# A searched order of work, and transposes and tile results in shared PSUM banks, in a three-layer mixture-of-experts and attention kernel

## The chip, the cores and the metric

The kernel runs on one core of a Trainium2 chip. The metric is device time in microseconds (us) for one execution of the whole program; lower is better. Engines: TensorE (PE, with its weight loads as PEld), VectorE (DVE), ScalarE (ACT), GpSimd (POOL) and SyncE (SP). They run side by side, each through its own queue in order, and wait for each other on semaphores.

## What is computed

```python
x = x + 0.5 * ffn(layernorm(x))
x = x + attn(layernorm(x))
x = x + 0.5 * ffn(layernorm(x))

def ffn(x):
    shared = (silu(x @ shared_gate.T) * (x @ shared_up.T)) @ shared_down.T
    probs = sigmoid(x @ router_w.T + routing_bias)
    scores, indices = top_k(probs, 2)          # of 8 experts, scores normed to sum 1
    w = scores scattered to (tokens, 8)
    g = silu(einsum('th,ehi->tei', x, gate_w)); u = einsum('th,ehi->tei', x, up_w)
    return shared + einsum('tei,eih,te->th', g * u, down_w, w)

def attn(x):                                    # 8 heads of 16, rope on q and k
    kv = einsum('bshd,bshe->bhde', k, v)        # linear attention: no S x S matrix
    num = q @ kv * scale + v.sum(1); den = q @ k.sum(1) * scale + S
    o = num / den + depthwise_conv(v, 5 taps)
    return (o * (x @ Wg.T)) @ Wo.T
```

x is 8 blocks of 512 tokens of width 128, all in float32. An expert's inner width is 256. The weights are the same in both FFNs.

## The kernel before

**Groups and tiles.** The 8 blocks go in two groups (g = 0, 1) of 4 blocks, through two FFNs (f = 0, 1) with attention between them, so there are four pairs (f, g), called groups below. For each group `route` (L449) turns the scores into a list of 39 tiles of 128 token places, each tile of one expert. `tile_lane` (L656) does a tile: GpSimd gathers its 128 rows from DRAM (`xg`), TensorE transposes them (`px`) and ACT copies them out (`xT`); one 128x512 matmul pair gives gate and up (`pgu`); ACT takes the silu (`sg`), DVE multiplies (`hh`); TensorE transposes twice (`ph`), ACT copies (`hT`); two accumulating matmuls give the tile's result (`py`), ACT copies it (`y`), and GpSimd scatters it to DRAM (`yd`). With all 39 tiles of a group done, `combine` (L728) loads the results (`yy`) and adds them, weighted, to the residual x. `shared` (L616) is the shared expert for one block: four steps of `pgu_s`, `sg_s`, `gu_s`, then eight matmuls `py_s` and an update of x. `attention` (L760) is one block's attention, and `prep` (L420) the layernorm, its transposes (`pxn`) and the router's logits (`pl`).

**What sets the order.** All these pieces are generators. A piece stops at each `Want`, which names the buffers, tensors or gate that it needs next. `run_lanes` (L206) takes, again and again, the lane with the earliest start by the planner's own clock; `rank` decides between lanes that could start at the same time. The planner's clock is `Order.note` (L80), which holds a written-in length for every kind of instruction, and `ready`, `used` and `free_at`, which say by a tile's name when it can be read and when its buffer comes free. What a lane issues is put on the engines' queues in that order; the semaphores between them follow from the tiles that instructions read and write. Ranks before are short formulas in g, f, block and tile (the last loop of the kernel).

**PSUM before.** The rings are made at L264. `gu` has 2 tiles of a whole bank (for `pgu` and `pgu_s`), `tr` 2 tiles of half a bank each (for `px` and `ph`), `y` one tile (for `py`), and `side` 3 banks for all else. In the built program each of these tiles has a bank of its own: 2 + 2 + 1 + 3 = 8.

```python
    for tag, bufs, shape, space in (
        ("gu", 2, [P, 2 * I], PSUM), ("tr", 2, [P, 2 * P], PSUM), ("y", 1, [P, D], PSUM),
        ("side", 3, [P, S], PSUM), ("xg", 8, [P, D], None), ("xT", 3, [P, P], None),
...
            rank = lane.rank if lane.want.rank is None else lane.want.rank
            key = (max(t, now), rank)
```

Nearly all instructions are issued through one helper, `Eng.call`, and so have line 158 in the profile; they are told apart by their tiles' names.

Of the kernel before, what the change touches and what calls it, by code (L numbers as in the profile page):

```python
# [8 lines left out]
F32 = mybir.dt.float32  # L9
# [25 lines left out]
EW = 2 * I + NI * D  # L35


SHORT = {"DVE": 2.5, "POOL": 2.0}


class Order:
# [3 lines left out]
    def __init__(self):  # L45
        self.t = {"PE": 0.0, "DVE": 0.0, "ACT": 0.0, "POOL": 0.0, "SP": 0.0,
                  "bytes": 0.0}
        self.ready, self.used, self.rings, self.open = {}, {}, {}, set()
        self.by = {}
        self.mark = 0.0  # L50
        self.table = None


    def ring(self, tag, pool, bufs, shape):
        self.rings[tag] = [pool, bufs, shape, []]

    def free_at(self, tag):
        _, bufs, _, names = self.rings[tag]
# [7 lines left out]
    def take(self, tag, name):  # L66
        pool, bufs, shape, names = self.rings[tag]
        at = self.free_at(tag)
        assert at is not None, (tag, name)
        t = pool.tile(shape, F32, tag=tag, name=name)  # L70
        names.append(t.tensor.name)
        self.open.add(t.tensor.name)
        self.used[t.tensor.name] = at
        return t

    def free(self, *tiles):
        for t in tiles:
            self.open.remove(t.tensor.name)

    def note(self, eng, op, a, k):  # L80
        aps = [v for v in list(a) + list(k.values()) if isinstance(v, bass.AP)]
        out, ins = aps[0], aps[1:]
        if k.get("out") is not None:
            out = k["out"]
            ins = [v for v in aps if v is not out]
        for v in k.values():
            if isinstance(v, bass.IndirectOffsetOnAxis):
                ins.append(v.ap)
        n = 1
        for d in out.shape[1:]:  # L90
            n *= d
        lag = 0.15
        if eng == "PE":
            if op == "transpose":
                cost = 0.125
            elif ins[0].dtype != F32:
                cost = 0.08
            else:
                cost = max(0.25, 0.00168 * n)
        elif op == "dma_start":  # L100
            cost, lag = 0.08, 2.2
        elif op == "indirect_dma_start":
            cost, lag = 1.25, 1.6
        elif eng == "DVE":
            cost = 0.13 + (0.0006 if out.dtype not in (F32, mybir.dt.int32) else 0.00105) * n
            if op == "bn_stats":
                cost = 0.2
            elif op == "bn_aggr":
                cost = 0.08
            elif op == "scalar_tensor_tensor":  # L110
                cost += 0.08
            elif op == "tensor_reduce":
                cost = 0.36 if ins[0].shape[-1] > 1 else 0.25
        elif eng == "ACT":
            cost = 0.16 + 0.00083 * n
            if op == "activation" and k.get("bias") is not None:
                cost += 0.12
            f = a[2] if op == "activation" and len(a) > 2 else None
            if f in (AF.Silu, AF.Sigmoid) and f != self.table:
                cost += 1.3  # L120
                self.table = f
        else:
            cost = 1.03 if op == "tensor_tensor" else 0.2
        start = self.t[eng]
        for v in ins:
            name = v.tensor.name
            who, end = self.by.get(name, (None, 0.0))
            start = max(start, end if who == eng else self.ready.get(name, 0.0))
        o = out.tensor.name
# [12 lines left out]
        for v in ins:  # L142
            nm = v.tensor.name
            self.used[nm] = max(self.used.get(nm, 0.0), end + 0.1)
        self.mark = max(self.mark, end + lag)

# [27 lines left out]
class Lane:  # L174


    def __init__(self, rank, gen, behind=None):
        self.rank, self.gen, self.want, self.marked = rank, gen, Want(), 0.0
        self.behind = behind

    def at(self, order):

        w = self.want
        if w.gate is not None and not w.gate():
            return None
        t = self.marked if w.mark else 0.0
        for tag in w.tags:
            f = order.free_at(tag)
            if f is None:
                return None  # L190
            t = max(t, f)
        for v in w.on:
            t = max(t, order.ready.get(v.tensor.name, 0.0))
        q = w.queue or self.behind
        if q:
            t = max(t, order.t[q] - SHORT[q])
        return t

    def step(self, order):
        order.mark = 0.0  # L200
        self.want = next(self.gen, None)
        self.marked = order.mark
        return self.want is not None


def run_lanes(order, lanes):  # L206


    while lanes:
        now = order.t["PE"]  # L210
        best = None
        for lane in lanes:
            t = lane.at(order)
            if t is None:
                continue
            rank = lane.rank if lane.want.rank is None else lane.want.rank
            key = (max(t, now), rank)
# [9 lines left out]
def kernel(  # L227
# [34 lines left out]
    pe, dve, act = Eng(od, nc.tensor, "PE"), Eng(od, nc.vector, "DVE"), Eng(od, nc.scalar, "ACT")  # L262
    pool, sp = Eng(od, nc.gpsimd, "POOL"), Eng(od, nc.sync, "SP")
    for tag, bufs, shape, space in (  # L264
        ("gu", 2, [P, 2 * I], PSUM), ("tr", 2, [P, 2 * P], PSUM), ("y", 1, [P, D], PSUM),
        ("side", 3, [P, S], PSUM), ("xg", 8, [P, D], None), ("xT", 3, [P, P], None),
        ("sg", 3, [P, I], None), ("hh", 3, [P, I], None), ("hT", 3, [P, NI * P], None),
        ("ys", 5, [P, D], None),
    ):
        kw = {"space": space} if space else {}  # L270
        od.ring(tag, ctx.enter_context(tc.tile_pool(name=f"r_{tag}", bufs=bufs, **kw)), bufs, shape)


    xres = [const.tile([P, C, D], F32, tag=f"x{b}", name=f"x{b}") for b in range(NB)]
# [341 lines left out]
    def shared(G, bl, turn):  # L616
        b = G.g * GB + bl
        u = f"s{G.u}_{bl}"
        yield Want(gate=lambda: bl in G.xnT and len(finished) >= turn - 1 and groups[0, 0].scored
                   and (G.f == 0 or groups[1, NG - 1].prepared == GB))  # L620
        xnT = G.xnT[bl]
        yield Want("gu", "sg", on=[xnT])
        gu = keep.tile([P, NI, S], F32, tag="sgu", name=f"gu_{u}", bufs=2)
# [291 lines left out]
    def in_stage(n, bl, gen):  # L915
        yield Want(gate=lambda: stage[bl] == n)
        yield from gen
        stage[bl] += 1

    def first_prep(g, bl):  # L920
        yield Want(on=[xres[g * GB + bl]], gate=lambda: g == 0 or groups[0, 0].begun >= LEAD + 4 * bl)
        yield from prep(groups[0, g], bl)

    def middle(g, bl):

        yield from combine(groups[0, g], bl)
# [12 lines left out]

    lanes = [Lane(0, q_lane())]  # L940
    for g in range(NG):
        for f in range(2):
            G = groups[f, g]
            lanes.append(Lane(5 + g, route(G, 2 * f + g)))
            for j in range(NT):
                lanes.append(Lane(40 + 2 * (2 * f + g) + j / NT, tile_lane(G, j)))
        for bl in range(GB):
            lanes.append(Lane(10 + 60 * g + bl, in_stage(g, bl, first_prep(g, bl))))
            lanes.append(Lane(20 + 4 * g + bl, in_stage(NG + g, bl, middle(g, bl)), "DVE"))
            lanes.append(Lane(60 + 4 * g + bl, in_stage(2 * NG + g, bl, out_lane(g, bl))))  # L950
# [72 lines left out]
```

## Time and profile before

| what | value |
|---|---|
| median of 3 runs | 645.43 us (642.58 to 649.0) |
| the profiled execution's own time | 648.35 us |
| its span in the profile | 646.6 us |
| mean granted TensorE clock | 0.917 |
| indirect transfers issued by GpSimd | 312 (156 gathers, 156 scatters) |
| first gather | starts at 42.9 us |
| loads of a group's results (yy), by group | from 186.8, 331.2, 509.3 and 628.9 us |

The page lists busy time by engine, the span in 40 slices (busy tenths, and the granted clock of TensorE in tenths), and the chain of work that ended last, followed back from the end. "issue" is time in which an engine waited for nothing that the profile shows. Other views give the waits by who waited for whom, the busy time in chosen stretches, and the instructions in order of time. Durations there come from the one profiled execution.

### The profile page before, as it was taken

What the parts mean: (1) busy time and instruction counts of PE and PEld (TensorE: products, weight loads), DVE (VectorE), ACT (ScalarE), POOL (GpSimd) and SP (SyncE); (2) the same over time, 40 slices, a digit from 0 to 9 for tenths busy, and PEclk for the clock granted to TensorE, in tenths of its full rate; (3) what the DMA queues carried; (4) which work ended last, traced back from release to release, by engine and by line L of the source; (5) the groups of instructions that cost most, each with busy time, mean ns of one, the idle gap of its engine ahead of it and who ended that gap; (6) DMA issues with size and microseconds to landing.
All of it is one profiled execution on the core that took longest, in us unless ns stands there. A gap on an engine that the chain in (4) does not pass through costs nothing.

```text
span 646.6 us, 9387 instructions
## 1 busy us (share of the span) xinstructions
PE 518.8 (80%) x2668; PEld 369.4 (57%) x2668; DVE 315.9 (49%) x1014; ACT 293.8 (45%) x933; POOL 347.2 (54%) x353
## 2 busy tenths in 40 slices
PE   3777979778889999997647889989686877887793
PEld 3565756455665767675334467667364655555573
DVE  5573222273227678773545677782562243232235
ACT  1214446533446665454405655454533444453343
POOL 5026566656665666466355455356456656566530
PEclk9989788997899999998766999997789979899997
DMA  9802122111141112112141011102111421111206
GB/s 247 230 13 58 33 57 68 38 35 37 38 148 48 38 32 58 33 53 48 18 147 40 14 33 45 36 28 65 30 29 46 155 61 58 48 50 46 41 15 190
DMA packets 41825, 40.59 MB, mean 63 GB/s; under 512 B 7085, under 2 KB 37049, under 8 KB 41776
## 3 DMA queue, kind: packets, MB, share of 16 engines
q0 software_dynamic: 9984, 18.65, 11.2%
q1 hardware_dynamic: 30944, 20.95, 10.8%
q10 hardware_dynamic: 848, 0.40, 0.3%
q8 instruction: 23, 0.38, 0.2%
q14 instruction: 26, 0.21, 0.1%
HBM read 25.28 MB, written 16.52 MB: 65 GB/s over the span
## 4 chain that ended last, share of the span: by engine, by line
PE 65%; DVE 11%; issue 9%; ACT 8%; DMA 3%; another core or an unknown queue 2%; POOL 1%; DVEq 0%; SPq 0%; ACTq 0%; POOLq 0%
PE pgu L158 20%; PE py L158 11%; PE pgu_s L158 7%; PE ph L158 6%; PE px L158 4%; PE py_s L158 3%; PE pl_f L158 3%; PE pkv L158 2%; DMA xg<-xnd,idx 2%; ACT hT L158 1%; PE pf L158 1%; PE pxn_f L158 1%; PE pi L158 1%; PE pkk L158 1%
## 5 line engine op out<-in xcount | busy, mean ns | idle before, releaser
L158 POOL DMA_INDIRECT yd<-y,dst x156 | 161.0, 1032 | 153.9 <-ACT y L158 87.7
L158 POOL DMA_INDIRECT xg<-xnd,idx x156 | 156.3, 1002 | 78.8 <-issue 35.0
L158 PE MATMUL pgu<-wx,xT 128*128 x312 | 180.9, 670 | 13.8 <-issue 8.7
L158 PEld LDWEIGHTS py<-wx,hT 128*128 128x128 f32 x624 | 95.5, 206 | 91.1 <-issue 41.8
L158 DVE TENSOR_TENSOR hh<-pgu,sg 128x256 f32<-128x256 f32 x156 | 65.2, 423 | 161.1 <-ACT sg L158 109.9
L158 PE MATMUL py<-wx,hT 128*128 x624 | 108.0, 299 | 35.2 <-issue 18.0
L158 ACT ACTIVATE sg<-pgu 128x256 f32<-128x256 f32 x156 | 60.0, 386 | 87.6 <-PE pgu L158 63.3
L158 ACT COPY hT<-ph 128x256 f32<-128x256 f32 x156 | 56.9, 371 | 48.7 <-PE ph L158 20.6
L158 ACT COPY y<-py 128x128 f32<-128x128 f32 x156 | 41.4, 265 | 75.0 <-PE py L158 33.9
L158 PEld LDWEIGHTS pgu<-wx,xT 128*128 128x128 f32 x312 | 53.6, 212 | 24.9 <-issue 16.8
L158 PE MATMUL ph<-ident,hh 128*128 128x128 f32 x312 | 62.3, 291 | 6.6 <-ACT xT L158 5.1
L158 PE MATMUL px<-ident,xg 128*128 128x128 f32 x156 | 40.3, 299 | 32.6 <-ACT hT L158 17.9
L158 PEld LDWEIGHTS ph<-ident,hh 128*128 128x128 f32 x312 | 43.0, 153 | 36.4 <-issue 18.7
L158 DVE TENSOR_TENSOR gu_s<-pgu_s,sg_s 128x256 f32<-128x256 f32 x64 | 26.7, 423 | 75.9 <-ACT sg_s L158 50.1
L158 PEld LDWEIGHTS px<-ident,xg 128*128 128x128 f32 x156 | 22.6, 150 | 53.2 <-ACT hT L158 24.2
L158 ACT COPY xT<-px 128x128 f32<-128x128 f32 x156 | 38.8, 273 | 21.6 <-PE px L158 15.0
L158 ACT ACTIVATE sg_s<-pgu_s 128x256 f32<-128x256 f32 x64 | 24.4, 384 | 52.2 <-PE pgu_s L158 23.5
L158 PE MATMUL pgu_s<-xnT_f,sgw 128*128 128x256 f32 x128 | 41.9, 411 | 0.6 <-DVE hh L158 0.2
L158 PE MATMUL pgu_s<-xnT_f,suw 128*128 128x256 f32 x128 | 40.4, 399 | 0.0
L158 POOL TENSOR_TENSOR rstd_f<-ve_f,neghalf 128x4 f32<-128x4 f32 x16 | 16.7, 1044 | 33.6 <-DVE ve_f L158 31.6
L158 PE MATMUL py_s<-sdw,gu_s 128*128 128x128 f32 x256 | 31.9, 277 | 1.6 <-DVE gu_s L158 1.6
L158 PEld LDWEIGHTS py_s<-sdw,gu_s 128*128 128x128 f32 x256 | 30.6, 194 | 2.6 <-DVE gu_s L158 1.8
(143 smaller groups left out, 656.9 us busy)
## 6 DMA issues: line engine op xcount, KB each, us to landing
yy<-yd SPq DMA_DIRECT2D x16, 512.0 KB
xnd<-xn_f SPq DMA_DIRECT2D x16, 256.0 KB
xg<-xnd,idx POOLq DMA_INDIRECT x156
yd<-y,dst POOLq DMA_INDIRECT x156
x<-in_x_dram SPq DMA_DIRECT2D x8, 256.0 KB
out_dram<-x SPq DMA_DIRECT2D x8, 256.0 KB
wx<-in_gate_w_dram SPq DMA_DIRECT2D x1, 1024.0 KB
wx<-in_up_w_dram SPq DMA_DIRECT2D x1, 1024.0 KB
```

The costliest lines, as they stand in the source:

```text
L158: r = f(*a, **k)
```

## The change

Three things are changed together.

1. **PSUM.** `gu` gets a third bank. The banks of `tr` and `y` go; two banks, `bank0` and `bank1`, take their place. `tr` becomes a ring of three places of half a bank: both halves of bank 0 and the first half of bank 1. `y` becomes a ring of two places, the third and fourth quarter of bank 1. `Order` keeps such a place's state by the place (`name`, `ring_of`), not by the bank.
2. **Ranks.** Every lane takes its rank from a table, and for tiles, shared blocks and the middle lanes each piece of a lane can add to it (`ADD`). The tables are numbers found by trial.
3. **Gates.** A shared block starts only when a number of tiles from `AFTER` has begun (for the eight blocks of the second FFN 122, 120, 68, 42, 84, 128, 41 and 115, for those of the first 0, 0, 0, 0, 13, 1, 31 and 0). The old gate, that the second FFN's shared blocks wait until the last group's blocks are prepared, goes. The order of the shared blocks among each other stays bound by `len(finished) >= turn - 1`, so the blocks of the second FFN, behind the first two gates, start when 120 tiles have begun.

The planner's lengths for GpSimd's elementwise work also change a little. What each instruction computes is the same, and so is the number of instructions.

```diff
+RANK = {
+    "q_lane": [
+        -62.33,
+    ],
+    "route": [
+        42.26, -96.58, 12.75, -83.93,
+    ],
...
+AFTER = [
+    0, 122, 0, 120, 0, 68, 0, 42, 13, 84, 1, 128, 31, 41, 0, 115,
+]
...
+    def ring_of(self, tag, places):
+
+        for t, first, _ in places:
+            self.shared.setdefault(t.tensor.name, []).append([first, None])
+            self.shared[t.tensor.name].sort(key=lambda part: part[0])
+        self.rings[tag] = [None, len(places), places, []]
+
+    def name(self, v):
+
+        parts = self.shared.get(v.tensor.name)
+        if parts is None:
+            return v.tensor.name
+        return [who for first, who in parts if first <= v.offset % S][-1]
...
-        t = pool.tile(shape, F32, tag=tag, name=name)
-        names.append(t.tensor.name)
-        self.open.add(t.tensor.name)
-        self.used[t.tensor.name] = at
+        if pool is None:
+            tensor, first, n = shape[len(names) % bufs]
+            t = tensor[:, first : first + n]
+            for part in self.shared[tensor.tensor.name]:
+                if part[0] == first:
+                    part[1] = name
+        else:
+            t = pool.tile(shape, F32, tag=tag, name=name)
+            name = t.tensor.name
+        names.append(name)
+        self.open.add(name)
+        self.used[name] = at
         return t
...
-            cost = 1.03 if op == "tensor_tensor" else 0.2
+            cost = 1.03 if n < 100 else 0.21 + 0.00207 * n
...
+    def rank_now(self):
+        own = self.rank if self.want.rank is None else self.want.rank
+        return own + (self.add[self.n] if self.n < len(self.add) else 0.0)
...
-        ("gu", 2, [P, 2 * I], PSUM), ("tr", 2, [P, 2 * P], PSUM), ("y", 1, [P, D], PSUM),
+        ("gu", 3, [P, 2 * I], PSUM),
...
+    bank = ctx.enter_context(tc.tile_pool(name="bank", bufs=1, space=PSUM))
+    banks = [bank.tile([P, S], F32, tag=f"b{n}", name=f"bank{n}") for n in range(2)]
+    od.ring_of("tr", [(banks[n // 2], n % 2 * 2 * P, 2 * P) for n in range(3)])
+    od.ring_of("y", [(banks[-1], 2 * P, P), (banks[-1], 3 * P, P)])
...
-        yield Want(gate=lambda: bl in G.xnT and len(finished) >= turn - 1 and groups[0, 0].scored
-                   and (G.f == 0 or groups[1, NG - 1].prepared == GB))
+        yield Want(gate=lambda: bl in G.xnT and len(finished) >= turn - 1 and groups[0, 0].scored)
...
-                lanes.append(Lane(40 + 2 * (2 * f + g) + j / NT, tile_lane(G, j)))
+                lanes.append(
+                    Lane(tiles_at[f * NG + g] + j / 40, tile_lane(G, j), add=ADD["tile"])
+                )
...
-                lanes.append(Lane(80 + 8 * f + 4 * g + bl, shared(groups[f, g], bl, (f * NG + g) * GB + bl)))
+                lanes.append(
+                    Lane(next(rank["shared"]), shared(groups[f, g], bl, (f * NG + g) * GB + bl),
+                         add=ADD["shared"], gate=begun(next(after)))
+                )
```

More of the change, by code (lines that the diff above doesn't have):

```diff
@@ L35 @@
 EW = 2 * I + NI * D
-SHORT = {"DVE": 2.5, "POOL": 2.0}
+RANK = {
[5 more added lines that the diff above has]
+    ],
+    "first": [
+        -10.65, -4.01, -21.58, -57.52, 51.38, 69.46, 67.86, 85.67,
+    ],
+    "mid": [
+        18.79, 11.7, 26.03, 28.66, 38.54, 25.61, 27.43, 11.7,
+    ],
+    "out": [
+        42.09, 4.55, 59.73, 122.09, 132.48, -14.93, -0.46, 83.82,
+    ],
+    "shared": [
+        80.65, 88.09, 59.59, 89.79, 60.46, 97.66, 135.22, 101.96, 65.72, 55.98, 94.12, 171.42,
+        91.54, 79.83, 98.56, 67.09,
+    ],
+    "tile": [
+        16, 43.86, 78.77, 52.12,
+    ],
+}
+ADD = {
+    "mid": [
+        0, 4.12, 0, 1.19, 0, -33.91, -9.15, -70.78, 1.76, -1.4, -0.73, 0.87, -7.22, -12.47,
+        14.32, 0, 0.49, -31.74, 0, 0.26, 2.81, -1.33, -2.51, 13.43, -0.86, -44.2, -0.06, -0.94,
+        0, -2.24, -11.81, 46.28,
+    ],
+    "tile": [
+        0, 0.33, -40.05, 0, 0, 0, 13.55, 0,
+    ],
+    "shared": [
+        0, -0.16, 0, -11.33, 4.43, -0.01, -1.23, -2.28,
+    ],
+}
+AFTER = [
+    0, 122, 0, 120, 0, 68, 0, 42, 13, 84, 1, 128, 31, 41, 0, 115,
+]
+SHORT = {"DVE": 2.5, "POOL": 2}
 class Order:
@@ L49, in __init__ @@
         self.by = {}
+        self.shared = {}
         self.mark = 0.0
@@ L77, in free, with busy @@
         for t in tiles:
-            self.open.remove(t.tensor.name)
+            self.open.remove(self.name(t))
+    def busy(self, eng, op, cost):
+        self.t[eng] += cost
     def note(self, eng, op, a, k):
@@ L122, in note @@
         else:
-            cost = 1.03 if op == "tensor_tensor" else 0.2
+            cost = 1.03 if n < 100 else 0.21 + 0.00207 * n
         start = self.t[eng]
         for v in ins:
-            name = v.tensor.name
+            name = self.name(v)
             who, end = self.by.get(name, (None, 0.0))
             start = max(start, end if who == eng else self.ready.get(name, 0.0))
-        o = out.tensor.name
+        o = self.name(out)
         start = max(start, self.used.get(o, 0.0))
@@ L142, in note @@
         for v in ins:
-            nm = v.tensor.name
+            nm = self.name(v)
             self.used[nm] = max(self.used.get(nm, 0.0), end + 0.1)
@@ L174, with __init__ @@
 class Lane:
-    def __init__(self, rank, gen, behind=None):
+    def __init__(self, rank, gen, behind=None, add=(), gate=None):
         self.rank, self.gen, self.want, self.marked = rank, gen, Want(), 0.0
-        self.behind = behind
+        self.behind, self.add, self.gate, self.n = behind, add, gate, 0
+    def rank_now(self):
+        own = self.rank if self.want.rank is None else self.want.rank
+        return own + (self.add[self.n] if self.n < len(self.add) else 0.0)
     def at(self, order):
         w = self.want
+        if self.n == 0 and self.gate is not None and not self.gate():
+            return None
         if w.gate is not None and not w.gate():
@@ L192, in at @@
         for v in w.on:
-            t = max(t, order.ready.get(v.tensor.name, 0.0))
+            t = max(t, order.ready.get(order.name(v), 0.0))
         q = w.queue or self.behind
@@ L200, in step @@
         order.mark = 0.0
+        self.n += 1
         self.want = next(self.gen, None)
@@ L215, in run_lanes @@
                 continue
-            rank = lane.rank if lane.want.rank is None else lane.want.rank
-            key = (max(t, now), rank)
+            key = (max(t, now), lane.rank_now())
             if best is None or key < best[0]:
@@ L938, in q_lane, with begun @@
         swap_q()
-    lanes = [Lane(0, q_lane())]
+    rank = {kind: iter(of) for kind, of in RANK.items()}
+    def begun(n):
+        return lambda: sum(G.begun for G in groups.values()) >= n
+    after = iter(AFTER)
+    tiles_at = list(RANK["tile"])
+    lanes = [Lane(next(rank["q_lane"]), q_lane())]
     for g in range(NG):
@@ L943 @@
             G = groups[f, g]
-            lanes.append(Lane(5 + g, route(G, 2 * f + g)))
+            lanes.append(Lane(next(rank["route"]), route(G, 2 * f + g)))
             for j in range(NT):
-                lanes.append(Lane(40 + 2 * (2 * f + g) + j / NT, tile_lane(G, j)))
+                lanes.append(
+                    Lane(tiles_at[f * NG + g] + j / 40, tile_lane(G, j), add=ADD["tile"])
+                )
         for bl in range(GB):
-            lanes.append(Lane(10 + 60 * g + bl, in_stage(g, bl, first_prep(g, bl))))
-            lanes.append(Lane(20 + 4 * g + bl, in_stage(NG + g, bl, middle(g, bl)), "DVE"))
-            lanes.append(Lane(60 + 4 * g + bl, in_stage(2 * NG + g, bl, out_lane(g, bl))))
+            lanes.append(Lane(next(rank["first"]), in_stage(g, bl, first_prep(g, bl))))
+            lanes.append(
+                Lane(next(rank["mid"]), in_stage(NG + g, bl, middle(g, bl)), "DVE", ADD["mid"])
+            )
+            lanes.append(Lane(next(rank["out"]), in_stage(2 * NG + g, bl, out_lane(g, bl))))
             for f in range(2):
-                lanes.append(Lane(80 + 8 * f + 4 * g + bl, shared(groups[f, g], bl, (f * NG + g) * GB + bl)))
+                lanes.append(
+                    Lane(next(rank["shared"]), shared(groups[f, g], bl, (f * NG + g) * GB + bl),
+                         add=ADD["shared"], gate=begun(next(after)))
+                )
     run_lanes(od, lanes)
```

## Prediction

> **What bounds the kernel now.** I read the engine totals, the granted clock and the chain that ended last, then busy time by stage, then TensorE's waits, then a stretch of the timeline.
>
> ```profile
> PE 518.8 (80%) x2668; PEld 369.4 (57%) x2668; DVE 315.9 (49%) x1014; ACT 293.8 (45%) x933; POOL 347.2 (54%) x353
> ...
> PEclk9989788997899999998766999997789979899997
> ...
> PE 65%; DVE 11%; issue 9%; ACT 8%; DMA 3%; another core or an unknown queue 2%; POOL 1%; DVEq 0%; SPq 0%; ACTq 0%; POOLq 0%
> ```
>
> TensorE is busy for 80% of the span and makes 65% of the chain; no other engine passes 54%. Its queue sets the time for most of the run, and its 128 idle us (646.6 - 518.8) are what an order can win.
>
> ```profile
> 0.00:43.00 43.00, 26.18 (x126) 21.72 (x126) 26.39 (x112) 8.49 (x16) 8.87 (x22) 0.96 0.65 180
> 43.00:194.00 151.00, 124.19 (x638) 87.94 (x638) 52.94 (x176) 66.62 (x216) 94.64 (x95) 0.91 0.20 56
> ...
> 307.00:339.00 32.00, 16.03 (x84) 11.56 (x85) 17.00 (x60) 9.14 (x24) 13.57 (x15) 0.72 0.30 79
> ...
> 614.00:647.00 33.00, 22.32 (x133) 18.23 (x133) 15.06 (x39) 13.70 (x45) 5.87 (x6) 0.87 0.32 100
> ```
>
> Columns: stretch, length, busy (count) of PE, PEld, DVE, ACT, POOL, clock. From 43 to 194 us, tiles of the first group, TensorE works 124 of 151 us. GpSimd's 95 instructions take 1.0 us each and the next starts 0.30 us later ("issue" in its rows), so 95 x 1.3 = 124 us: a second engine near its limit. Of the 128 idle us, 17 lie before 43 us and 11 after 614 us, so 100 in between.
>
> ```profile
> PE py L158 <- issue: 18.0, 13, 2.8
> PE px L158 <- ACT hT L158: 17.9, 11, 4.6
> PE py L158 <- ACT hT L158: 13.9, 13, 2.8
> ...
> PE py L158 <- ACT y L158: 3.1, 2, 2.6
> ...
> PE pgu L158 <- DVE hh L158: 1.3, 2, 1.2
> ```
>
> Columns: waits in us, times, longest. The largest named cause is ACT's copy hT, 31.8 us. For the product hh that frees a gate-up bank TensorE waits 1.3 us, for y 3.1.
>
> ```profile
> 592.85 0.38 PE L158 MATMUL ph<-ident,hh 128*128 128x128 f32 x2
> 592.96 0.30 PEld L158 LDWEIGHTS pgu<-wx,xT 128*128 128x128 f32 x2
> 593.05 0.38 ACT L158 ACTIVATE sg_s<-pgu_s 128x256 f32<-128x256 f32 x1 [0.48 <-PE pgu_s L158]
> 593.07 1.02 PE L158 MATMUL pgu<-wx,xT 128*128 x2
> 593.33 0.37 ACT L158 COPY hT<-ph 128x256 f32<-128x256 f32 x1
> ...
> 593.93 0.61 PE L158 MATMUL py<-wx,hT 128*128 x4
> 594.27 0.30 PEld L158 LDWEIGHTS pgu<-wx,xT 128*128 128x128 f32 x2
> 594.38 0.59 PE L158 MATMUL pgu<-wx,xT 128*128 x1
> ```
>
> From start to start, at full clock: the two transposes ph 0.22 us, pgu 0.86, the two py 0.45; px, half of ph, 0.11. A tile keeps TensorE for 0.11 + 0.86 + 0.22 + 0.45 = 1.64 us, and GpSimd for two transfers, 2.6 us. The same stretch prices a wait for a copy. TensorE could have gone on at 593.07; the copy began 0.26 later; after its end TensorE needs some 0.16 (0.05 to the weight load, 0.11 to the matmul, as 592.96 to 593.07). Copy plus 0.42 us is thus what must lie between a write and the next write that waits for its copy: 0.69 for px (0.273 by its row), 0.79 for ph (0.371), 0.69 for py (0.265).
>
> **The change part by part.** The instructions are the same in number on every engine (1,712 matmuls, 312 indirect transfers); order, buffers and waits differ. I laid both built orders out on TensorE's queue with those start-to-start times, 439 us in all at full clock.
>
> *Shared banks.* Before, each of the two tr tiles and the y tile has a bank alone. After, bank 0 holds two tr parts, bank 1 one tr part and both y parts. In the build a write to a part waits for ACT's copy out of the other parts of that bank too: 287 of TensorE's waits are for another part (176 in bank 1, 111 in bank 0). The planner's bookkeeping goes by part, so it places work as if five places were free where two are. [...]
>
> For each write I took TensorE work since the end of the write before it in its bank, against copy + 0.42. Before, 27 of 465 writes fall short, by 9.0 us. After, 172 of 466 fall short, by 107.8 us (27, 25, 26 and 30 in the four groups' stages); 40 times two py stand directly behind each other in one bank. That adds 98.8 us. It holds if ACT is free: 145 more short waits, ACT busy 45%, its instructions near 0.38 us, so each meets up to 0.38 us of other work; I take 0.45 x 0.38 = 0.17, 25 us (ends 0 and 55). Added on TensorE: 124 us (99 to 154). Queued behind each stalled write is everything on TensorE, so ACT's and VectorE's next inputs and GpSimd's scatter of y come later as well.
>
> How much of it lands? Where TensorE makes the chain (65%), and there a stall ahead of an existing idle moment only moves it: 100 idle us of the 571 between, 17%. So 0.65 x 0.83 = 0.54, 67 us. Ends: 0 if GpSimd's 2.6 us a tile covers it all, 1 if TensorE is the only limit.
>
> *Third gate-up bank.* With two, the work between reuses was short 14 times, by 2.6 us in all; with three never: -3 us, as the 1.3 us row says too.
>
> *Second y part.* It lies in the bank of the first, so the 3.1 us wait for y is not removed: 0.
>
> *Order.* The median TensorE work between ph and its py grows from 0.97 to 2.31 us, so an ACT that is late hurts less. At most all of hT's 31.8 us goes, at least nothing; half, -16, since px's 17.9 of it becomes a bank wait of the kind above.
>
> *Head.* Parts of three shared blocks now run through the first routing instead of two. Until the last routing matmul, DVE gets 4 more gu_s at 0.42 and one x update at 0.69: 2.4 us on the chain that releases the first gather at 42.9 us. TensorE's extra work there, six matmuls of 0.43 and 8 of 0.22, lies mostly in the head's 17 idle us: +3. The 7 us of TensorE work thus taken from later stages are worth 0.65 x 7 = -4.5.
>
> *Tail.* After the last py stand 12.3 us of shared work instead of 9.6, and this work ends before the last x updates: +3.
>
> The dropped gate on the second FFN's shared blocks changes nothing: their new gates hold them until 120 tiles have begun. The order of gathers and scatters on GpSimd stays within a few places, SP's transfers are the same, ACT loads its tables 8 times in both. The gap at 307 to 339 us stays: the last py of the second group and the third group's first px stand at 226 and 228 us of TensorE work in both.
>
> Sum: 67 - 3 - 16 + 3 - 4.5 + 3 = +49.5. On the profiled span: 646.6 + 49.5 = 696; that run took 648.4 and the median of three is 645.4, so 3 less: 693 us.
>
> **The rivals.** *All of it lands.* If ACT's copies are as late as the 31.8 us of hT waits suggest (before, all shortfalls that I can count, gate-up and data waits included, are 24 us, and the seen idle is 100), the 124 us come whole: 124 - 17.5 = +106 less 3, about 749. For it: 80% busy, 65% of the chain. Against it: GpSimd at 124 of 151 us has slack of its own to give. The clock could go the same way: if stalls took it from 0.917 to 0.85, 518.8 x (0.917/0.85 - 1) = 41 us more busy time.
>
> *Hidden.* GpSimd paces the tiles, and the stalls fill idle time that is there anyway. TensorE needs 1.64 us per tile plus the shared work, against 2.6 us on GpSimd. With 0.12 to 0.27 of the 124 us landing (15 to 33) and the other terms as above (-17.5) it gives -2 to +16 us, less 3: 642 to 659.
>
> *Faster.* One mechanism: the longer distance from ph to py ends all hT waits (-31.8, with -3 - 4.5 + 6 from above -33), and GpSimd's pace hides nine tenths of the bank stalls (+12): 646.6 - 21 - 3 = about 622. It decides where less than 33/124 = 0.27 of the stalls lands. Against it: 65% of the chain is TensorE, only 1% GpSimd.
>
> **How the numbers follow.** The forecast (stalls land by 0.4 to 0.75, 660 to 725) gets 0.60, all landing (725 to 770) 0.17, hidden 0.10, faster 0.13. Predicted 693. The range leaves out a tenth at each end, part of the faster case and part of the all-landing one: 630 to 742. About 1%, 6.5 us, is what a measurement of this kernel can tell from no change: the three runs before lie 6.4 us apart. Faster by more 0.13, within 0.08 (most of the hidden case), slower 0.79.
>
> **What would show it.** Right: TensorE's waits before px, ph and py on ACT's copies (xT, hT, y) grow from about 45 us to over 100, many of them 0.3 to 0.8 us long; its busy time stays near 519 while its idle time grows in all four tile stages; the waits on hh for a gate-up bank vanish; the first gather starts at 45 to 47 us. Wrong: short bank waits in number but a span below 650, GpSimd's idle time falling instead; or a clock below 0.88, which would make the loss another one than the one I costed.

## The result: 761 us, and the profile after

The changed kernel takes 761.33 us (median of 4 runs, 754.75 to 763.55) against 646.36 us for the kernel before (4 runs): a ratio of 1.177, interval 1.167 to 1.186. The forecast of 693 us had the sign; the time lies 68 us above it and 19 us above the end of the range. The profiled execution spans 759.9 us, 113.3 more than before.

From the page of the changed kernel, the rows that answer to those of before:

```profile
PE 562.8 (74%) x2668; PEld 388.5 (51%) x2668; DVE 316.3 (42%) x1014; ACT 303.4 (40%) x933; POOL 346.0 (46%) x353
...
PEclk9999796798978789998756979889879798989898
...
PE 23%; ACT 4%; issue 3%; another core or an unknown queue 2%; DVE 1%; DVEq 0%; ACTq 0%
```

TensorE has the same 2668 records and is busy for 44.0 us more; its idle time grew from 127.8 to 197.1 us, 69.3 more. The two make the 113.3. VectorE and GpSimd are busy as before. The clock row has many more dips: the mean fell from 0.917 to 0.871. The chain can't be set against the one of before, since its links add up to a third of the span only.

By stage (stretch, length, busy and count of PE, PEld, DVE, ACT, POOL, clock, DMA share, GB/s):

```profile
0.00:47.00 47.00, 34.82 (x181) 30.25 (x182) 31.42 (x129) 10.96 (x23) 12.01 (x25) 0.96 0.61 168
47.00:220.00 173.00, 128.36 (x590) 86.57 (x589) 48.35 (x163) 63.98 (x202) 86.11 (x87) 0.84 0.17 48
...
350.00:400.00 50.00, 33.64 (x156) 23.65 (x154) 23.09 (x81) 19.48 (x55) 17.99 (x18) 0.69 0.23 58
...
720.00:760.00 40.00, 27.20 (x155) 21.64 (x155) 17.95 (x46) 17.23 (x57) 7.89 (x8) 0.93 0.31 93
```

Head, seam and tail are much as they were. The loss is in the tile stages: in the first group's, TensorE idles for 44.6 of 173 us where it idled for 27 of 151, at a clock of 0.84.

TensorE's waits (us in total, times, longest):

```profile
PE bank L227 <- ACT y L227: 39.3, 53, 3.6
PE bank L227 <- ACT xT L227: 36.0, 41, 4.8
PE bank L227 <- ACT hT L227: 35.8, 44, 4.1
PE bank L227 <- issue: 22.5, 17, 5.0
PE pgu L227 <- ACT xT L227: 10.7, 3, 8.8
...
PE bank L227 <- DVE hh L227: 1.1, 1, 1.1
```

The waits on ACT's copies came as forecast: 39.3 + 36.0 + 35.8 + 10.7 = 122 us, from about 45. Two things were not forecast. Some waits are far too long for a copy of 0.27 to 0.37 us (8.8, 5.0, 4.8), and the clock fell. Sorted by length, TensorE's gaps of 0.3 to 0.8 us grew from 23 (12.4 us) to 119 (53.1 us), and those over 3.5 us from 4 (19.3 us) to 9 (43.3 us), the wait at the program's start left out.

The longest of these gaps, in order of time (start, length, engine, operation; idle time before and its releaser in brackets):

```profile
203.06 1.73 PE L227 MATMUL py_s<-sdw,gu_s 128*128 128x128 f32 x14
...
204.62 0.27 PE L227 MATMUL bank<-ident,xg 128*128 128x128 f32 x1
...
205.16 0.59 PE L227 MATMUL pgu_s<-xnT_f,suw 128*128 128x256 f32 x2
205.86 1.02 POOL L227 DMA_INDIRECT yd<-y,dst  x1 [0.30 <-issue]
207.18 0.97 POOL L227 DMA_INDIRECT xg<-xnd,idx  x1 [0.30 <-issue]
208.45 0.95 POOL L227 DMA_INDIRECT xg<-xnd,idx  x1 [0.30 <-issue]
209.71 1.02 POOL L227 DMA_INDIRECT yd<-y,dst  x1 [0.30 <-issue]
211.03 0.98 POOL L227 DMA_INDIRECT xg<-xnd,idx  x1 [0.30 <-issue]
...
214.17 0.69 DVE L227 SCALAR_TENSOR_TENSOR x<-py_s,x 128x512 f32<-128x512 f32 x1 [10.62 <-remote]
214.20 0.27 ACT L227 COPY xT<-bank 128x128 f32<-128x128 f32 x1 [9.08 <-remote]
...
214.52 1.22 PE L227 MATMUL pgu<-wx,xT 128*128 x1 [8.76 <-ACT xT L227]
```

VectorE's update of x waits, in the build, for the last py_s alone, and that ended by 204.8 us in the records; ACT's copy waits for the transpose of xg alone, recorded at 204.62. Both start at 214.2, within 0.03 us of each other, released by nothing that this view can name ("remote"). In between, of the five engines only GpSimd works until 212 us: the last five of twelve indirect transfers that follow each other at 1.3 us, from 196.9 to 212.0 us. This isn't a wait for a bank.

The trace also holds the time of each update of a semaphore, and these show what was late. TensorE's semaphore is updated at 204.83 us and then only at 214.15, 214.18 and 214.24; by their order these three stand for the last py_s, the transpose of xg and the products pgu_s, and VectorE and ACT start 0.02 us after the first and the second. By the records that work ended at 204.8, 204.9 and 205.8 us, and pgu_s alone takes 0.87 us from start to start, so it can't have been computed between two of these updates: TensorE had done the work, and its updates came some 9 us late. Those of the DMA queues went on, 33 of them in between. VectorE and ACT are thus not stopped by themselves; they wait for TensorE.

I call a stretch of over 1 us after the first gather in which TensorE, VectorE and ACT are all idle a standstill. After, there are 19, 41.0 us in all; all 19 overlap the time from the fifth transfer of an unbroken run of six or more on GpSimd (at most 0.4 us from one to the next) to 1 us after the run's end, and such times are 141 us of the span. Before, there were 16, 24.4 us, 15 of them so placed, and such times were 125 us. Runs of nine and more: 1 before, with 10 transfers; 9 after, with 99.

### The profile page after: what moved, and what is told of

Same layout as the page of the kernel before. It is cut to its first block, busy times and chain, and to the rows that moved or that the text cites. A ratio compares the mean times of both kernels' runs of the same rounds, so it can differ in the third digit from the quotient of the medians.

```text
span 759.9 us, 9448 instructions
## 1 busy us (share of the span) xinstructions
PE 562.8 (74%) x2668; PEld 388.5 (51%) x2668; DVE 316.3 (42%) x1014; ACT 303.4 (40%) x933; POOL 346.0 (46%) x353
## 5 line engine op out<-in xcount | busy, mean ns | idle before, releaser
L227 POOL DMA_INDIRECT yd<-y,dst x156 | 158.8, 1018 | 211.4 <-ACT y L227 159.8
L227 PE MATMUL pgu<-wx,xT 128*128 x312 | 181.5, 681 | 16.5 <-ACT xT L227 10.7
L227 PE MATMUL bank<-wx,hT 128*128 x624 | 116.9, 315 | 58.4 <-ACT xT L227 21.4
L227 PEld LDWEIGHTS bank<-wx,hT 128*128 128x128 f32 x624 | 94.4, 213 | 95.5 <-ACT xT L227 31.8
L227 PE MATMUL bank<-ident,hh 128*128 128x128 f32 x312 | 67.0, 304 | 37.5 <-ACT y L227 12.4
L227 ACT COPY hT<-bank 128x256 f32<-128x256 f32 x156 | 57.0, 370 | 73.5 <-PE bank L227 37.0
L227 ACT COPY y<-bank 128x128 f32<-128x128 f32 x156 | 41.5, 266 | 109.0 <-PE bank L227 72.8
L227 PEld LDWEIGHTS bank<-ident,hh 128*128 128x128 f32 x312 | 42.5, 156 | 80.1 <-issue 28.8
L227 PE MATMUL bank<-ident,xg 128*128 128x128 f32 x156 | 46.3, 315 | 47.5 <-ACT hT L227 15.6
L227 PEld LDWEIGHTS pgu<-wx,xT 128*128 128x128 f32 x312 | 57.4, 218 | 36.8 <-issue 18.4
L227 PEld LDWEIGHTS bank<-ident,xg 128*128 128x128 f32 x156 | 23.2, 153 | 83.4 <-ACT hT L227 27.9
L227 ACT COPY xT<-bank 128x128 f32<-128x128 f32 x156 | 39.8, 267 | 31.3 <-PE bank L227 16.6
L227 POOL TENSOR_TENSOR rstd_f<-ve_f,neghalf 128x4 f32<-128x4 f32 x16 | 16.6, 1040 | 70.2 <-DVE ve_f L227 62.3
L227 PE MATMUL pgu_s<-xnT_f,suw 128*128 128x256 f32 x128 | 43.3, 423 | 0.0
```

The costliest lines, as they stand in the source:

```text
L227: r = f(*a, **k)
```

## The experiments

**Theory** at first: the short bank waits land harder than I counted, and the clock falls with them. **Rival**: the order of the work costs time by itself. After four runs the standstills gave a third theory: GpSimd's unbroken sequences of indirect transfers hold up the other engines, and the new order meets or makes more of them. All runs in one table; the ratio is to the kernel before on the same chip, which took 638 to 648 us there. The last column adds up, from the first gather to the last matmul, the times of over 1 us from the last matmul that ended and carries an update to TensorE's next update ("late updates"). Some updates are missing from the traces, 13 to 16% of TensorE's in the two main ones. Most others come 0.01 us after the recorded end, and neither VectorE nor ACT has a late one between the first gather and the program's end in any of these traces.

| run | us | ratio (interval) | clock | standstills, us | late updates, us |
|---|---|---|---|---|---|
| before (profile) | | 1 | 0.917 | 24.4 | 40.8 |
| changed (profile) | 761.3 | 1.177 (1.167 to 1.186) | 0.871 | 41.0 | 61.1 |
| e1 order only | 720.1 | 1.129 (1.120 to 1.138) | 0.887 | 40.3 | 77.0 |
| e2 banks only | 678.7 | 1.065 (1.058 to 1.073) | 0.935 | 10.4 | 16.6 |
| e3 tables only | 652.4 | 1.021 (1.014 to 1.028) | 0.903 | 24.2 | 46.4 |
| e4 planner knows | 696.0 | 1.094 (1.084 to 1.103) | 0.886 | 33.6 | 49.3 |
| e5 order, own places | 733.9 | 1.133 (1.125 to 1.141) | 0.875 | 48.0 | 85.8 |
| e6 changed, pause 0.1 | 760.1 | 1.170 (1.160 to 1.181) | 0.875 | 37.0 | 68.5 |
| e12 changed, pause 0.23 | 725.7 | 1.119 (1.113 to 1.124) | 0.893 | 21.0 | 45.5 |
| e7 changed, pause 0.34 | 660.2 | 1.020 (1.012 to 1.028) | 0.946 | 0 | 5.5 |
| e15 changed, 0.34 at gathers | 717.1 | 1.111 (1.102 to 1.120) | 0.907 | 15.2 | 37.2 |
| e16 changed, 0.34 at scatters | 719.4 | 1.112 (1.099 to 1.125) | 0.908 | 20.9 | 48.0 |
| e14 changed, 1.44 one in four | 684.7 | 1.059 (1.049 to 1.069) | 0.931 | 5.7 | 0 |
| e8 before, pause 0.1 | 652.4 | 1.005 (1.001 to 1.009) | 0.912 | 29.7 | 47.0 |
| e17 before, pause 0.23 | 626.0 | 0.985 (0.975 to 0.995) | 0.922 | 18.2 | 26.8 |
| e9 before, pause 0.34 | 618.9 | 0.957 (0.954 to 0.959) | 0.935 | 8.9 | 12.8 |
| e13 before, pause 0.67 | 768.0 | 1.189 (1.180 to 1.198) | 0.855 | 101.6 | 0 |
| e10 banks only, pause 0.34 | 656.3 | 1.018 (1.010 to 1.026) | 0.930 | 8.4 | 1.1 |
| e11 own places, pause 0.34 | 644.5 | 0.994 (0.992 to 0.997) | 0.939 | 2.9 | 13.8 |
| e18 tables, pause 0.34 | 623.6 | 0.979 (0.971 to 0.987) | 0.942 | 18.6 | 4.5 |

**e1: the order alone.** The change's order on every engine; gate-up on two banks, transposes on two, results on one, as before. The planner still counts three, three and two; where two gate-up tiles are open, a third takes a bank that is free at that time.

```diff
-        ("gu", 3, [P, 2 * I], PSUM),
...
+    od.ring_of("gu", [(banks[n], 0, S) for n in range(2)], 3, [(banks[2], 0, S)])
+    od.ring_of("tr", [(banks[2 + n], 0, 2 * P) for n in range(2)], 3)
+    od.ring_of("y", [(banks[4], 0, P)], 2)
```

> The changed kernel's order of instructions on every engine, kept exactly, but with PSUM placed as before: two gate-up banks, two tr banks, one y bank, none of them shared. Counted shortfall of the bank waits (work between two writes to a bank against copy + 0.42 us): 46.7 us, against 9.0 before and 107.8 after. If the bank waits are the cause, time follows that count: 646 + 115 x (46.7 - 9.0)/98.8 = 690 us. If the order itself is the cause, it stays near 761 us. If the third gate-up bank and the y part were worth anything, it is above both.

720 us, 82 over before. Only part can be bank waits: the gate-up bank now waits 21.5 us for VectorE, which the change's third bank avoids.

**e2: the banks alone.** The order of before, three gate-up banks and the shared parts of the change; the planner counts two, two and one.

```diff
+    od.ring_of("gu", [(banks[n], 0, S) for n in range(3)], 2)
+    od.ring_of("tr", [(banks[3 + n // 2], n % 2 * 2 * P, 2 * P) for n in range(3)], 2)
+    od.ring_of("y", [(banks[4], 2 * P, P), (banks[4], 3 * P, P)], 1)
```

> The order of before, kept exactly on every engine, with PSUM placed as after: three gate-up banks, tr in three parts and y in two parts of two banks. Counted shortfall 73.3 us. Bank waits as the cause: 646 + 115 x 64.3/98.8 = 721 us, with the granted clock below 0.90. Order as the cause: 646 us, since no instruction has moved.

679 us, 40 over before (638.35 there). From its page and its waits:

```profile
PE 517.8 (77%) x2668; PEld 364.2 (54%) x2668; DVE 317.6 (47%) x1014; ACT 303.1 (45%) x933; POOL 347.4 (52%) x353
```

```profile
PE bank L188 <- ACT hT L188: 37.9, 36, 4.3
PE bank L188 <- ACT y L188: 29.9, 41, 2.9
...
PE bank L188 <- ACT xT L188: 15.3, 18, 2.8
```

This is what the forecast described: 83 us of waits on copies, TensorE busy as before. The clock did not fall (0.935). The late updates fell from 40.8 to 16.6 us, so the 40 us may be what is left of a larger price. My count for this kernel: 64.3 us more shortfall, 92 more short writes with 0.17 each for ACT's queue, 80 us; 40 of them landed, a share of 0.50, where I had put 0.54.

**e3: the tables alone**, planned on the rings of before; ranks, ADD, gates and costs as in the change.

```diff
-        ("gu", 3, [P, 2 * I], PSUM),
+        ("gu", 2, [P, 2 * I], PSUM), ("tr", 2, [P, 2 * P], PSUM), ("y", 1, [P, D], PSUM),
...
-    od.ring_of("tr", [(banks[n // 2], n % 2 * 2 * P, 2 * P) for n in range(3)])
-    od.ring_of("y", [(banks[-1], 2 * P, P), (banks[-1], 3 * P, P)])
```

> The tables of ranks, the added ranks and the gates of the change, with the rings of before (the planner knows that it has two gate-up banks, two tr banks, one y bank). Counted shortfall 12.3 us. Bank waits as the cause: within 2% of before, about 650 us. Order as the cause (the table suits the planner's model and not the chip): 670 us or more.

2% slower. The ranks are not the bulk of the loss; what the planner was told of free places is, or what comes of it.

**e4: the planner knows.** The changed kernel with a place counted free only when the whole bank is.

```diff
+        if self.rings[tag][0] is None:
+            tensor = self.rings[tag][2][len(names) % bufs][0]
+            for _, who in self.shared[tensor.tensor.name]:
+                at = max(at, self.used.get(who, 0.0), self.ready.get(who, 0.0))
```

> The changed kernel, except that the planner counts a place in a shared bank as free only when the copies out of all parts of that bank are done. Counted shortfall 60.8 us. If the cost is that the planner does not see the bank waits: 646 + 115 x 51.8/98.8 = 706 us, or less. If the cost lies in having two banks for what had three, whatever the planner knows: 750 us or more.

696 us: within the first expectation, and no proof of it. The counted shortfall fell by 47 us (107.8 to 60.8), the gaps over 3.5 us from 9 to 5, and the clock stayed at 0.886. Two causes moved together.

**e5: the order on places of its own.** As e1, but with three gate-up banks; the side tiles make do with two.

```diff
+    od.ring_of("gu", [(banks[n], 0, S) for n in range(3)], 3)
...
+    od.ring_of("side", [(banks[6 + n], 0, S) for n in range(2)], 3, [(banks[5], 0, S)])
```

> The change's order on every engine, with three gate-up banks as its planner counts them, and the transposes (2) and tile results (1) in banks of their own (the side tiles have 2 banks in place of 3); the counted bank shortfall is 46.7 us, as in the run of the order alone, but the gate-up bank's waits on VectorE (21.5 us there) should be gone. If the order itself is the loss: the stretches in which TensorE, ScalarE and VectorE are all idle for over 1 us stay near 40 us in sum (41.1 after, 24.4 before), the clock stays below 0.90, 690 to 710 us. If the order costs only what its bank waits cost: 46.7 x 0.6 = 28 us over before, 660 to 670 us, clock above 0.91.

734 us, more than either theory gave. The 21.5 us of waits for VectorE's gu_s are gone, and nothing was gained (ratios 1.129 and 1.133). Standstills are 48.0 us. Here the bank theory fell: its 28 us for the counted waits are far from 86 us over before.

**e6, e7, e8 and e12: pauses on GpSimd.** Nothing moves on any engine; one memset of a scratch tile stands ahead of each of the 312 indirect transfers.

```diff
+        nc.gpsimd.memset(scratch, 0.0)
         pool.indirect_dma_start(
             out=xg, out_offset=None, in_=G.xn_d,
...
+        nc.gpsimd.memset(scratch, 0.0)
         put = pool.indirect_dma_start(
```

The scratch tile is 128x1 (e6, e8), 128x128 (e12) or 128x256 (e7).

> The changed kernel, every instruction in its place, with one memset of 128x1 (0.1 us) on GpSimd ahead of each of its 312 indirect transfers. Theory: unbroken runs of six and more indirect transfers on GpSimd hold up the semaphores between the other engines (nearly all stretches with TensorE, ScalarE and VectorE idle at once lie in such runs or at their ends), so breaks in the runs bring these stretches from 41 us to 20 or less, the clock over 0.90, and the time under 730 us. Rival: the runs only happen beside the stall, or a break this short changes nothing: 745 to 765 us, the stretches at 35 to 45 us.

> As the run with short pauses, with a memset of 128x256 (an estimated 0.3 us between the 0.20 of 128x128 and more) ahead of each indirect transfer. Theory: at least as few stalls as with the short pause, under 730 us. Rival: GpSimd's queue is the limit in its bursts (1.3 us a transfer), so 0.3 us more on each makes the bursts a quarter longer and the kernel slower: 760 to 800 us.

> The kernel before, every instruction in its place, with the memset of 128x1 ahead of each indirect transfer. Theory of the runs: its 24 us of stretches with three engines idle shrink to 12 or less, 620 to 632 us. Rival: no change, 636 to 645 us.

> The changed kernel with a memset of 128x128 (0.20 us) ahead of each indirect transfer: transfers every 1.33 us, an estimate from 1.28 without and 1.45 with 0.34 us. If the pace of the transfers decides: between 760 and 660 us, near 720, with 15 to 30 us of stretches with three engines idle. If a threshold lies between the two: one of the ends, 655 to 675 or 745 to 765 us.

The short memset fits in the 0.30 us between two transfers: closest together they still start every 1.30 us, and nothing changed by more than 0.6% (e6, e8). Breaking the run by another instruction is thus not what counts. The memset of 0.34 us makes them start every 1.50 us, and not every 1.45 as I had put it when I wrote down what I expected of e9 and e12:

```profile
80.10 0.99 POOL L227 DMA_INDIRECT xg<-xnd,idx  x1 [0.16 <-PE pgu L227]
81.09 0.32 POOL L799 MEMSET scratch<- 128x256 f32 x1
81.59 1.00 POOL L227 DMA_INDIRECT yd<-y,dst  x1 [0.17 <-issue]
```

The changed kernel falls by 100 us. From the page of e7:

```profile
PE 514.9 (79%) x2668; PEld 360.2 (55%) x2668; DVE 317.2 (48%) x1014; ACT 304.0 (46%) x933; POOL 446.5 (68%) x665
...
PEclk9999999999997899999957998979989999999998
```

and its waits on TensorE and on GpSimd:

```profile
PE bank L227 <- ACT hT L227: 27.6, 36, 2.1
PE bank L227 <- ACT y L227: 26.5, 47, 2.2
PE bank L227 <- ACT xT L227: 25.9, 38, 3.7
```

```profile
POOL yd L227 <- ACT y L227: 40.2, 28, 5.9
```

GpSimd has 100 us more work and the kernel is 100 us shorter. No standstill is left, and the late updates fall from 61.1 to 5.5 us. TensorE is busy for 47.9 us less, at a clock of 0.946. The bank waits stay: 127 gaps of 0.3 to 0.8 us, 55.7 us, where the changed kernel had 119 and 53.1. GpSimd's wait for y ahead of a scatter falls from 159.8 to 40.2 us. The memset of 128x128 took 0.23 us, not the 0.20 that I expected; with it (1.39 from start to start) a good third of the gain is there (e12), so between 1.30 and 1.50 us the effect comes by degrees.

**e9, e10 and e11: the same pauses of 0.34 us** on the kernel before, on e2 and on e5.

> The kernel before, every instruction in its place, with the memset of 128x256 (0.34 us) ahead of each indirect transfer, so that these follow each other at 1.45 us and not at 1.28. Theory: GpSimd's fast runs of indirect transfers also stall the kernel before (its long gaps over 1.5 us are 70.6 us, 39.8 in the changed kernel with these pauses; 31 cold clock windows of 1.7 us against 20), so it gains about 31 + 19 us: 595 to 615 us. Rival: only the changed order meets the stall, and the pauses cost the kernel before their own time: 645 to 665 us.

> The order of before on the change's shared banks, with the long pauses on GpSimd. Theory: with the stalls away the price of the shared banks stands alone, about the 25 to 43 us that the gaps of 0.3 to 0.8 us grew by: 30 to 45 us more than the kernel before with the long pauses (630 to 655 us). Rival: the bank waits were cover for the stalls or the other way round, and with the pauses the banks cost under 15 us.

> The change's order with three gate-up banks and its transposes and results in banks of their own, with the long pauses. Theory: the order's loss (734 us without pauses) was the stalls, so what is left over the kernel before with long pauses is the counted bank waits, 46.7 x 0.6 = 28 us: 620 to 645 us. Rival: the order is slow by itself, 680 us or more.

e10 and e11 are where their theory put them (656 against 655 at most, 645 at most), and before is 4 us above its own. The kernel before had the stall too and falls to 618.9 us, the fastest kernel of all here and better than both that were compared. From its page:

```profile
PE 505.7 (82%) x2668; PEld 361.9 (59%) x2668; DVE 316.5 (51%) x1014; ACT 294.2 (48%) x933; POOL 449.5 (73%) x665
```

With the stall away little is left of the loss: the banks cost 656.3 - 618.9 = 37 us, the order on places of its own 26, the whole change 660.2 - 618.9 = 41 (e7 ran on another chip; by the ratios it is 41 too). The first two aren't parts of a sum. The order on its own places has bank waits as well, since its planner counts three tr and two y places where there are two and one: 37.7 us of shortfall and 58 short writes, 48 us, of which the forecast's share of 0.54 makes 26. That the 26 us are these waits is a count that fits, not shown by a run.

**e13 and e17: the dose on the kernel before**: two memsets of 128x256 ahead of each transfer, and one of 128x128.

```diff
+        nc.gpsimd.memset(scratch, 0.0)
+        nc.gpsimd.memset(scratch, 0.0)
         pool.indirect_dma_start(
```

> The kernel before with two memsets of 128x256 (0.67 us) ahead of each indirect transfer, in place of one. If the single pause leaves stalls (9 us of stretches with three engines idle are still there): under 612 us. If it has removed them, the second only makes GpSimd slower (312 x 0.34 = 106 us more of its time): 620 to 660 us.

> The kernel before with a memset of 128x128 (0.20 us) ahead of each indirect transfer. The changed kernel had 35% of its gain from this pause, against the one of 0.34 us. If before follows the same line: 0.35 x 29 = 10 us less, 630 to 640 us. If before is also held by GpSimd's own time at 0.34 us, the shorter pause is as good or better: 610 to 622 us.

With 0.67 us the gathers are the limit, worse than I expected: 768 us. Two lines of e13, its chain and TensorE's first wait in the costliest groups:

```profile
PE 46%; DMA 15%; POOL 14%; issue 9%; ACT 7%; DVE 7%; POOLq 0%; DVEq 0%; SPq 0%; ACTq 0%
```

```profile
L158 PE MATMUL px<-ident,xg 128*128 128x128 f32 x156 | 46.1, 311 | 157.8 <-DMA xg<-xnd,idx 142.0
```

Its standstills are another kind: TensorE waits for gathers that come late, and no update of TensorE's is late. The range between stall and limit is narrow: by the ratios 0.23 us gives 1.5%, a third of the 4.3% of 0.34 us, as the first expectation of e17 has it (its 626 us lie under that expectation's 630 because before took 640 us on that chip), and 0.67 us loses 19%.

**e14, e15 and e16: what about the runs.** Four memsets ahead of every fourth transfer; the 0.34 us ahead of gathers alone; ahead of scatters alone. For the first, ahead of each transfer:

```diff
+        moved.append(0)
+        if len(moved) % 4 == 0:
+            for _ in range(4):
+                nc.gpsimd.memset(scratch, 0.0)
```

> The changed kernel with four memsets of 128x256 (1.35 us) ahead of every fourth indirect transfer: the same 105 us of pauses as the run with one ahead of each (660 us), in a quarter of the places. If the length of an unbroken run makes the stall: 650 to 675 us. If the pace from one transfer to the next makes it: 700 to 745 us, with over 15 us of stretches with three engines idle.

> The changed kernel with the pause of 0.34 us ahead of the 156 gathers alone. If the mean pace of the queue counts: about half of the gain of 100 us, 695 to 725 us. If the gathers carry the stall: 655 to 675 us; if the scatters do: 740 us or more.

> The changed kernel with the pause of 0.34 us ahead of the 156 scatters alone. If the mean pace of the queue counts: 695 to 725 us, as with the gathers alone. If the scatters carry the stall: 655 to 675 us; if the gathers do: 740 us or more.

Gathers and scatters are alike, the pauses of either kind bring some 42% of the gain: it isn't one kind. One long pause in four brings about three quarters: between the two expectations, nearer to that of the run's length. No run in it is longer than four. Inside the fours the transfers start every 1.30 us as in the changed kernel, and with the pause every 1.7 us on the mean (e7 1.50), since four memsets in one place use only one of the gaps of 0.30 us. Not one of TensorE's updates is late in it. What it lacks against e7 shows in another wait:

```profile
PE bank L227 <- DMA xg<-xnd,idx: 34.4, 29, 4.4
```

In e7 this is 7.9 us: the pauses of 1.44 us make gathers late, and all four standstills of e14 end with one. So the stall took both, the full pace and a run of more than four: fours at full pace (e14) have none of it (0 us of late updates), and long sequences at 1.50 us (e7) hardly any (5.5 us).

**e18: the tables with the pauses**, e3 with the memset of 128x256 ahead of each transfer.

> The change's rank tables, gates and costs, planned on the rings of before (2% slower than before without pauses), with the pause of 0.34 us ahead of each indirect transfer. If their loss was the stall: within 8 us of the kernel before with the same pauses (619), 610 to 627 us. If the order that the tables make is slow by itself: 630 to 640 us.

623.6 us is inside the first expectation, but on a chip on which before took 640 us and not 648. By ratio the tables are 2.3% slower than before with the same pauses (0.979 and 0.957, intervals apart), and without pauses they were 2.1% slower: the 2% aren't the stall, whose late updates fell to 4.5 us. Its profile shows another wait that grew:

```profile
PE px L227 <- DMA xg<-xnd,idx: 57.1, 43, 7.3
```

In e3 this wait is 14.6 us, in e9 15.2. These ranks leave little between a gather and its use: from the start of the gather to its tile's copy xT it is 4.9 us on the median, in e9 9.8, and 50 of 156 gathers have under 4 us (11 in e9).

## Why the prediction was right in sign and wrong in size

**Bank stalls, +67: the mechanism right, a little large.** The places cost 40 us without and 37 with the pauses in the order of before. For the changed kernel with pauses, 41 + 17.5 of the other terms would be 58 of 124 us, a share of 0.47 where I took 0.54; with the term for the order, which fell, at nothing it is 42.5 of 124, 0.34. By the planner's view the parts would have cost nothing; by the waits in the built program they cost the counted shortfall. The runs speak for the second: the shared places alone bring 83 us of waits on copies (e2) and 37 us of time (e10 against e9). Whether the chip needs these waits isn't shown, since every run has them where places share a bank.

**The failed step: "The order of gathers and scatters on GpSimd stays within a few places", and so no term for GpSimd.** The sentence holds (at most 7 places, 0.8 on the mean), but the conclusion fails. What counted is how closely the transfers follow each other in time (0.34 us between them took 100 us off, e7), and that changed: 99 of 312 stand in runs of nine and more, before 10. TensorE's updates came late by 61.1 us in sum against 40.8, and the clock was 0.871 against 0.917. The number of long runs doesn't give the size, though: the tables alone (e3) have 89 transfers in such runs, and 24.2 us of standstills as before. The profile of before held the sign, the same pace of 1.3 us and standstills of 24.4 us, and I read GpSimd's rows only as throughput: "slack of its own to give". The missing term is what the whole change costs without the pauses and with them, 115 - 41 = 74 us. It is more than the miss of 68; without it my sum of +49.5 would have been 8 us too high.

**Order, -16: fell.** With the stall away, the order on places of its own costs 26 us, which its counted bank waits can make up; a gain from the longer way from ph to py doesn't show. In the kernel with stalls the order was the larger part of the loss (+86 us in e5).

**Clock.** I said that a clock below 0.88 would make the loss another one than I costed; it was 0.871, and it was another one. "All of it lands" came within 12 us of the time and named a falling clock (0.85), but by luck, for a reason that fell: bank waits landed by half at most (0.50 in e2), and with e2's 83 us of them the clock was 0.935.

**Third gate-up bank, -3**: in the changed kernel the waits of pgu on hh are gone from the list (1.1 us is ph's wait for its own input). Nothing larger was hidden in it: e1 and e5 don't differ. **Head, +3**: the first gather starts at 42.7 us, not 45 to 47: 0. **Tail, +3**: from the last load of yy to the end 19.1 us (740.8 to 759.9), before 17.7: +1.4. **The seam** stayed, as said: 16 idle us at 350 to 400 us, at a clock of 0.69.

**Left open.** Why indirect transfers in close sequence hold up TensorE's updates, and only TensorE's. Ends of matmuls are modelled, but the updates that come 0.03 to 0.06 us apart after a standstill speak for late signals, not late matmuls. A backlog that grows over a run and drains in a pause would fit e7, e12 and e14; no run shows it. Also open is why e3, with its long runs, loses so little. That the new order makes runs longer is counted; that a late y ahead of a scatter dams up the gathers behind it, which then go in one run (GpSimd's wait for y: 87.7 before, 159.8 after, 40.2 with pauses), fits but is argued only.

## What to carry to other kernels

Look for moments in which engines stop and start together although the work that they wait for has ended in the records, see whose semaphore updates are late, and what the one engine that still works is doing; the longest such stall here, in which the updates came 9 us late, is booked as a wait of 8.8 us on ACT's copy xT. Where GpSimd issues indirect transfers back to back (1.30 us from start to start here), try a pause of a few tenths of a microsecond between them before counting waits elsewhere (0.34 us took 4.3% off the kernel before and 13% off the changed one), and find the dose by trial: with 0.67 us gathers came late, 142.0 us of waits and 19% more time (e13). Where the build makes a write to one part of a PSUM bank wait for copies out of its other parts, a planner that counts the parts apart plans work into waits, as here; the shared places cost 37 to 40 us in the order of before (e10, e2), and of the counted waits a third to a half landed.

## What the hardware showed that I had not expected

GpSimd's indirect transfers at 1.30 us from start to start, in runs of six and more, went with standstills of 1.0 to 8.4 us, in which TensorE's updates came late and VectorE and ACT waited for them; at 1.50 us, with a memset of 0.34 us between them, the changed kernel had no standstill and was 100 us faster.

The clock fell by windows of 3.41 us, and not with TensorE's mean load: with TensorE busy for 80% of the span the clock was 0.917 (before), with 77% 0.935 (e2). From the busy time in small stretches of the changed kernel, around the standstill at 110 us:

```profile
105.00:110.00 5.00, 5.00 (x33) 3.92 (x33) 1.27 (x3) 2.06 (x7) 3.78 (x5) 1.00 0.15 46
110.00:115.00 5.00, 0.34 (x4) 0.09 (x1) 0.69 (x1) 0.30 (x2) 3.78 (x5) 0.79 0.22 51
115.00:120.00 5.00, 3.44 (x11) 2.63 (x12) 0.00 (x0) 1.04 (x5) 1.98 (x2) 0.50 0.14 42
120.00:123.00 3.00, 3.00 (x7) 1.34 (x7) 0.44 (x2) 0.82 (x3) 0.00 (x0) 0.50 0.01 1
123.00:128.00 5.00, 3.58 (x16) 2.57 (x17) 1.35 (x6) 2.92 (x9) 0.00 (x0) 0.84 0.16 52
```

TensorE stops at 110.3 us; by the trace's rows of the clock it is at half from 112.9 to 123.1, some 10.2 us or three times 3.41, and so also while TensorE is already fully busy again. In the traces of before and after all dips go to half clock, and but for the last, at the program's end, they last one to six times 3.41 us and start whole multiples of 3.41 us apart. Before, 32 such windows ran at half clock (31 of them after the first gather, which what was expected of e9 counts at half of 3.41, 1.7 us each), after 58. TensorE was busy for 82.9 us of the first and for 143.8 us of the second; in such windows a matmul of pgu takes 0.85 us from start to start and outside 0.43, so, as an estimate from these figures, the clock makes half of the difference, 30 of the 44 us by which its busy time grew. What makes the other 14 isn't shown. In e7 it is busy for 46.2 us of such windows. Cut from the first row of the clock on into windows of 3.41 us, the changed kernel's trace shows what stood ahead of those at half clock: after windows in which TensorE was busy under half, 35 of 36 of the next ones were at half clock, after those over 80% 9 of 126, and after those between 14 of 53. The 80 gaps of 0.3 to 0.8 us in e2 went with a clock of 0.935 and a busy time of 517.8 us (before 518.8), so they cost little beyond their own time; a stop that left TensorE busy for under half of a window cost, as an estimate from these figures, up to half of the next one, 1.7 us, again.
